# Graph attention with residual norm on one Trainium2 core: VectorE adds the first two products with v in tiles 11 to 15 too

## The chip, the core and the metric

The kernel runs on one core of a Trainium2 chip. The core has five engines that run side by side, each with its own instruction queue: TensorE (PE, matrix products and transposes, with its weight load PEld), VectorE (DVE), ScalarE (ACT), GpSimd (POOL, which here issues the gathers) and SyncE (SP, which issues DMAs). They wait for each other on semaphores. The metric is the device time of one execution in microseconds (us).

## The reference

One layer: attention over the edges of a graph of 4096 nodes, width 512, 8 heads of 64, then a feed-forward block and a last layer norm. `adj` is about 0.4% full, so a node has some 17 neighbours.

```python
hs = layer_norm(h_source); ht = layer_norm(h_target)          # h_source is x
q = (ht @ Wq + bq).reshape(T, H, HD) / jnp.sqrt(HD)
k = (hs @ Wk + bk).reshape(S, H, HD)
v = (hs @ Wv + bv).reshape(S, H, HD)
logits = jnp.where(edge_mask[None] != 0, jnp.einsum('thd,shd->hts', q, k), NEG)
ctx = jnp.einsum('hts,shd->thd', softmax(logits), v).reshape(T, D)
ht = layer_norm(ht + ctx @ Wo + bo)
out = layer_norm(x + ht + gelu(ht @ W1) @ W2)
```

All of it is float32.

## The kernel before

**Sorted targets, gathered edges.** The attention is not dense. The first part of the run turns each row of `adj` into a list of neighbours, projects `x` to k and v (one row of 1024 floats per node, in `kvd` in DRAM) and sorts the 4096 targets by degree in two halves of 2048. A tile is 128 targets of like degree, one on each partition. The tile's cap is the largest number of neighbours that it makes room for. The first half (`CAPS_A`, 16 tiles) is worked on while the lists of the second half (`CAPS_B`) are still being made. `_order` puts the tiles into groups of two; counted in the order of work, tiles 0 to 15 are the first half with caps 11, 13, 14, 15, 15, 16, 17, 17, 18, 19, 19, 20, 22, 23, 24, 39, and tile 16 (cap 12) is the first of the second half. `NA` is 16. Groups are [0], [1, 2], and so on: [11, 12], [13, 14], [15, 16].

**A step.** A tile is worked in steps of up to three neighbours (`S = 3`, list `SG`). For each neighbour slot POOL gathers 128 rows of k and v, one per partition, into `kv`, a ring of 17 places in the first half and 20 in the second (`RING`). `request` and `issue` do this four or five steps ahead (`AHEAD`). Then

- DVE multiplies the k halves by the query (line 1223) and sums each head (line 1228): the logits;
- ACT takes the exponential (lines 1232 and 1241, no maximum is subtracted) and, in a step of three, multiplies the third slot's v half by its weights itself (`by_scalar`, line 1207);
- DVE multiplies the v halves of the other slots by their weights (`values`, line 1184);
- PE adds the slots up: it transposes each 128x128 block of each slot by a product with the identity, and the transposes of all slots of a tile accumulate in one PSUM bank, `cps` (line 1195). Four transposes per slot.

From tile `NA` on, DVE adds slot 1 to slot 0 first (line 1188), and PE then transposes slot 0 and the third slot alone. From tile 21 on (`DENSE`), in every other step of three, DVE adds the third slot as well (line 1191).

**Around the steps.** `front` makes a tile's query (transposes, then the product with Wq, line 1012, then line 1017 on DVE). `finish` normalises a finished tile, multiplies it by Wo (line 1116) and prepares the feed-forward input `h2T`. `feed` runs the feed-forward block of a group (lines 1328 and 1337, PE) and adds its result on DVE (line 1284).

**What sets the order.** `attention` and `feed` are generators. `_weave` runs them by turns after hand-set costs (60 for a group of two), so that the feed-forward block of an earlier group is interleaved with the attention steps of a later one. A scheduler in the framework then fixes the order of each engine's queue at build time; each queue runs strictly in that order.

Of `values`, the lines that count:

```python
nc.vector.tensor_tensor(v4, v4, p[...].to_broadcast([P, m, H, HD]), ALU.mult)     # line 1184
slots = list(range(n))
if m > 1 and i >= NA:
    nc.vector.tensor_add(kv[:, 0, D:], kv[:, 0, D:], kv[:, 1, D:])                 # line 1188
    slots.remove(1)
```

Here `n` is the number of slots of the step and `m` the number that DVE multiplies: `n - 1` in a step of three, else `n`.

Of the kernel before, what the change touches and what calls it, by code (L numbers as in the profile page):

```python
# [443 lines left out]
def adj_resnorm_kernel(  # L444
# [56 lines left out]
    NA, NBT = len(CAPS_A), len(CAPS_B)  # L501
# [31 lines left out]
    with tc.tile_pool(name="keep", bufs=1) as keep:  # L533
# [17 lines left out]
        with ExitStack() as late:  # L551
# [489 lines left out]
            def request(k):  # L1041


                ahead = AHEAD + (1 if k >= first_b else 0)
                while issued[0] <= min(k + ahead, len(SG) - 1):
# [121 lines left out]
            def attention():  # L1167
# [10 lines left out]
                def values(i, j0, n, kv, p, cps, after):  # L1178

                    m = n - 1 if n == S else n
                    v4 = kv[:, :m, D:].rearrange("p j (h d) -> p j h d", h=H)
                    nc.vector.tensor_tensor(v4, v4, p[:, j0:j0 + m, :].unsqueeze(3)  # L1184
                                            .to_broadcast([P, m, H, HD]), ALU.mult)
                    slots = list(range(n))
                    if m > 1 and i >= NA:
                        nc.vector.tensor_add(kv[:, 0, D:], kv[:, 0, D:], kv[:, 1, D:])
                        slots.remove(1)
                        if n == S and i >= DENSE and j0 // S % 2:  # L1190
                            nc.vector.tensor_add(kv[:, 0, D:], kv[:, 0, D:], kv[:, S - 1, D:])
                            slots.remove(S - 1)
                    for j in slots:
                        for c in range(KC):
                            nc.tensor.matmul(cps[:, c, :], kv[:, j, D + c * P:D + (c + 1) * P], ident,  # L1195
                                             is_transpose=True, start=j0 + j == 0 and c == 0,
                                             stop=j0 + n == TILES[i][1] and j == slots[-1],
                                             skip_group_check=True)
                    if after is not None:
                        tails.append(after)  # L1200
# [11 lines left out]
                for group in GROUPS:  # L1212
# [3 lines left out]
                    for i in group:  # L1216
                        cps = ps.tile([P, KC, P], F32, name="cps", bufs=2)
                        while k < len(SG) and SG[k][0] == i:
# [16 lines left out]
                            if pend:  # L1235
                                values(*pend.pop())
                                request(k)
# [9 lines left out]
                            yield cost * n  # L1247
                            k += 1
                values(*pend.pop())
                while tails:  # L1250
                    advance()
# [130 lines left out]

            WAIT = 40.0
            AHEAD = 4
            DENSE = 21
            UNIT = 60.0

# [103 lines left out]
```

## Time and profile before

| | us |
|---|---|
| median of 3 runs | 1815.97 |
| lowest and highest | 1810.59 and 1816.34 |
| the profiled execution, its own time | 1805.6 |
| its span (first to last instruction) | 1803.7 |

Some rows of the profile for the operations of a step (whole run; a duration is from an instruction's start to its end, and neighbours on one engine can overlap):

| line, engine | what | count | mean ns | busy us |
|---|---|---|---|---|
| 1223 DVE | k times query | 211 | 1674 | 351.5 |
| 1228 DVE | sum of heads | 211 | 1665 | 350.1 |
| 1184 DVE | v times weights | 211 | 1192 | 250.9 |
| 1188 DVE | slot 1 added to slot 0 | 101 | 682 | 68.7 |
| 1207 ACT | third slot's v times weights | 1520 | 336 | 390.4 |
| 1195 PE | transposes into `cps` | 1896 | 281 | 252.3 |
| 1328 PE | feed-forward, first product | 2176 | 368 | 465.6 |
| 1337 PE | feed-forward, second product | 1024 | 598 | 466.3 |
| 967 POOL | gathers of k and v | 603 | 1276 | 769.3 |

How to read such a profile: busy time is an average over stages with different limits, so a stage has to be looked at by itself. "Idle before, releaser" names what the engine was waiting for. A wait on an engine that is not the bottleneck costs nothing. Attention runs from about 300 us to 1690 us of the span; before it come the lists and the projections, after it the rest of the feed-forward blocks.

### The profile page before, as it was taken

The page shows a single profiled execution, that of the slowest core. Times are in us where ns is not written, and L with a number is a line of the kernel's source. Part 1 is how long each engine was busy: PE and PEld are TensorE (multiplying, and loading weights), DVE is VectorE, ACT ScalarE, POOL GpSimd, SP SyncE. Part 2 cuts the span into 40 slices and gives each one's busy share as a digit, 9 for nine tenths or more (in the row PEclk, how much of TensorE's full clock was granted, in tenths as well). Part 3 has the DMA queues.
Part 4 walks back from the last instruction along what each step waited for, and adds up shares of the span by engine and source line. Part 5 has one row for each costly group of instructions (what it writes and reads, how often), then busy time and mean ns, then how long its engine had stood idle before and what let it go on. Part 6 is the DMA issues. An engine that isn't in the chain of part 4 may idle for free. (4 is left out here: it accounts for less than half of the span.)

```text
span 1803.7 us, 22807 instructions
## 1 busy us (share of the span) xinstructions
PE 1666.8 (92%) x6918; PEld 1085.7 (60%) x6918; DVE 1452.4 (81%) x2688; ACT 1229.2 (68%) x3125; POOL 994.7 (55%) x834
## 2 busy tenths in 40 slices
PE   7989994597999979999999989999899999999997
PEld 3444442475766656776776756666566666666664
DVE  6999886899999837777979989978797898998200
ACT  5767554487987646767778868877787776887311
POOL 1000145666566676776677788877575757773101
PEclk9999997698999989999999999999999999999998
DMA  9999969989797647777879878786787867684000
GB/s 343 370 385 372 344 215 326 401 282 339 259 313 254 203 162 255 252 255 260 286 260 313 291 261 296 253 280 231 235 263 240 285 212 268 218 287 154 16 9 26
DMA packets 140268, 463.25 MB, mean 257 GB/s; under 512 B 16500, under 2 KB 21672, under 8 KB 140136
## 3 DMA queue, kind: packets, MB, share of 16 engines
q0 software_dynamic: 96656, 342.64, 56.1%
q1 hardware_dynamic: 35664, 95.98, 15.1%
q10 hardware_dynamic: 7816, 23.08, 3.3%
q8 instruction: 57, 0.93, 0.2%
q14 instruction: 75, 0.61, 0.1%
HBM read 430.75 MB, written 30.89 MB: 256 GB/s over the span
## 5 line engine op out<-in xcount | busy, mean ns | idle before, releaser
L967 POOL DMA_INDIRECT kv<-kvd,rec x603 | 769.3, 1276 | 340.3 <-PE cps L1195 138.1
L1337 PE MATMUL po<-w,gt 128*128 128x512 f32 x1024 | 466.3, 598 | 16.7 <-ACT gt L1331 16.7
L1328 PE MATMUL pf<-h2T,w 128*128 128x256 f32 (+1 forms) x2176 | 465.6, 368 | 0.3 <-ACT h2T L1147 0.3
L1328 PEld LDWEIGHTS pf<-h2T,w 128*128 128x128 f32 x2176 | 389.1, 191 | 64.4 <-issue 19.8
L1223 DVE TENSOR_TENSOR kv<-kv,tq 128x1536 f32<-128x1536 f32 (+2 forms) x211 | 351.5, 1674 | 61.8 <-DMA kv<-kvd,rec 53.3
L1207 ACT ACTIVATE kv<-kv,pa 128x64 f32<-128x64 f32 x1520 | 390.4, 336 | 4.1
L1228 DVE TENSOR_REDUCE lg<-kv 128x24 f32<-128x1536 f32 (+2 forms) x211 | 350.1, 1665 | 1.1
L1337 PEld LDWEIGHTS po<-w,gt 128*128 128x128 f32 x1024 | 188.6, 192 | 212.8 <-issue 194.2
L1195 PEld LDWEIGHTS cps<-ident,kv 128*128 128x128 f32 x1896 | 227.9, 145 | 110.1 <-issue 45.5
L1195 PE MATMUL cps<-ident,kv 128*128 128x128 f32 x1896 | 252.3, 281 | 44.2 <-DVE kv L1184 36.5
L1184 DVE TENSOR_TENSOR kv<-kv,p 128x1024 f32<-128x1024 f32 (+1 forms) x211 | 250.9, 1192 | 14.4 <-ACT p L1232 14.1
L687 POOL TENSOR_TENSOR n_rs<-n_ve,mhalf 128x2 f32<-128x2 f32 (+2 forms) x51 | 49.9, 979 | 322.6 <-DVE n_ve L680 170.8
L729 ACT ACTIVATE kv<-kv 128x1024 uint8<-128x1024 int32 x128 | 134.9, 1056 | 93.9 <-DMA kv<-in_adj_dram 41.4
L1331 ACT ACT_TABLE_LOAD x106 | 136.0, 1283 | 1.8
L1331 ACT ACTIVATE gt<-pf 128x512 f32<-128x512 f32 x128 | 76.4, 597 | 88.0 <-PE pf L1328 84.5
L736 DVE MAX8 cand<-kv 128x8 uint16<-128x103 uint16 (+1 forms) x640 | 131.4, 251 | 0.6
L930 PE MATMUL pq<-wk,h2T 128*128 128x512 f32 x256 | 120.8, 616 | 11.8 <-ACT tq L932 6.3
L1012 PE MATMUL t<-wq,tq 128*128 128x512 f32 x256 | 120.5, 615 | 8.2 <-ACT tq L1006 8.2
L930 PE MATMUL pq<-wv,h2T 128*128 128x512 f32 x256 | 115.4, 593 | 2.1 <-ACT kv L932 1.7
L1116 PE MATMUL t<-wo,rb 128*128 128x512 f32 x256 | 115.2, 593 | 0.0
L1232 ACT ACTIVATE p<-lg 128x24 f32<-128x24 f32 (+2 forms) x179 | 39.1, 218 | 105.5 <-DVE lg L1228 104.7
L930 PEld LDWEIGHTS pq<-wk,h2T 128*128 128x128 f32 x256 | 48.8, 197 | 69.8 <-issue 50.1
(161 smaller groups left out, 1606.2 us busy)
## 6 DMA issues: line engine op xcount, KB each, us to landing
kv<-in_adj_dram SPq DMA_DIRECT2D x128, 512.0 KB, 7.0
kvd<-tq ACTq DMA_DIRECT2D x24, 512.0 KB, 6.4
kv<-kvd,rec POOLq DMA_INDIRECT x603, 5.9
kv<-in_L_gnn_h_target_dram SPq DMA_DIRECT2D x32, 256.0 KB, 7.4
kv<-in_x_dram SPq DMA_DIRECT2D x15, 512.0 KB, 8.8
rest_d<-gid SPq DMA_DIRECT2D x32, 160.0 KB, 4.8
w<-in_L_gnn_W_dram SPq DMA_DIRECT2D x4, 1024.0 KB, 10.3
kvd<-kv ACTq DMA_DIRECT2D x8, 512.0 KB, 5.8
```

The source lines that it names most:

```text
L729: nc.scalar.activation(sg, a, AF.Sign, accum_out=dpart[:, i, h:h + 1])
L736: nc.vector.max(cand[:, h * SQ + s, :], wd[:, w0:w1])
L930: nc.tensor.matmul(pkv, hT[:, kc, j * P:(j + 1) * P], w[:, kc, :], start=kc == 0, stop=kc == KC - 1)
L967: nc.gpsimd.indirect_dma_start(out=dst, out_offset=None, in_=table[:, :], in_offset=bass.IndirectOffsetOnAxis(ap=idx, axis=0))
L1184: nc.vector.tensor_tensor(v4, v4, p[:, j0:j0 + m, :].unsqueeze(3) .to_broadcast([P, m, H, HD]), ALU.mult)
L1195: nc.tensor.matmul(cps[:, c, :], kv[:, j, D + c * P:D + (c + 1) * P], ident, is_transpose=True, start=j0 + j == 0 and c == 0, stop=j0 + n ...
L1207: newest[:] = [nc.scalar.mul(v, v, pa[:, hd:hd + 1]).ins]
L1223: nc.vector.tensor_tensor(kv[:, :n, :D], kv[:, :n, :D], tq[:, :D].unsqueeze(1).to_broadcast([P, n, D]), ALU.mult)
L1228: nc.vector.tensor_reduce(lg[:, :n, :], kv[:, :n, :D].rearrange("p j (h d) -> p j h d", h=H), AX.X, ALU.add)
L1328: nc.tensor.matmul(pf[:, k, :], w1[(f0 + k) // KC][:, kc, (f0 + k) % KC * P:((f0 + k) % KC + 1) * P], h2T[:, kc, :w], start=kc == 0, stop= ...
L1331: nc.scalar.activation(gt, pf, AF.Gelu_apprx_tanh)
L1337: nc.tensor.matmul(po[j], gt[:, k, j * P:(j + 1) * P], w2[(f0 + k) // KC][:, (f0 + k) % KC, :], start=False, stop=f0 + k == FC - 1, skip_g ...
```

## The change

The add of line 1188 starts at tile 11 instead of tile 16. A new constant names the tile.

```diff
@@ values
                     slots = list(range(n))
-                    if m > 1 and i >= NA:
+                    if m > 1 and i >= ADDS:
                         nc.vector.tensor_add(kv[:, 0, D:], kv[:, 0, D:], kv[:, 1, D:])
                         slots.remove(1)
                         if n == S and i >= DENSE and j0 // S % 2:
@@ constants
             AHEAD = 4
+            ADDS = 11
             DENSE = 21
```

`ADDS` is set further down in the kernel than `values` stands, but before the generators run, like `DENSE`. Tiles 11 to 15 have caps 20, 22, 23, 24 and 39.

## The prediction

> **What bounds the kernel now.** I read the page's first two parts for the overall load, then cut the span by the first exponential of each tile (line 1241 on ScalarE's timeline: tile 11 at 754.6 us, tile 13 at 850.3, tile 15 at 936.7, tile 17 at 1040.8, tile 19 at 1140.2, tile 21 at 1227.6, tile 23 at 1316.1, tile 25 at 1400.9) and took the busy time of each engine in each stretch, one stretch being one group of two tiles. Last came the timelines of PE and DVE around the tile borders.
>
> The page: span, load, and the 40 slices of PE and DVE.
> ```profile
> span 1803.7 us, 22807 instructions
> ...
> PE 1666.8 (92%) x6918; PEld 1085.7 (60%) x6918; DVE 1452.4 (81%) x2688; ACT 1229.2 (68%) x3125; POOL 994.7 (55%) x834
> ...
> PE   7989994597999979999999989999899999999997
> DVE  6999886899999837777979989978797898998200
> ```
> PE carries the most, and the last three slices have PE alone (DVE falls to 2, 0, 0): the feed-forward part of the last groups. PE's order is fixed, so whatever the middle gains or loses on PE arrives at the end undiminished.
>
> The busy time by group; columns are stretch, length, then busy microseconds and instructions of PE, weight load, DVE, ACT and POOL, granted clock, DMA share and rate.
> ```profile
> core 0: us, PE busy (x) PEld busy (x) DVE busy (x) ACT busy (x) POOL busy (x), PEclk, DMA share, GB/s
> 754.60:850.30 95.70, 92.86 (x436) 65.19 (x435) 74.59 (x84) 66.19 (x183) 67.48 (x56) 1.00 0.77 260
> 850.30:936.70 86.40, 85.31 (x406) 59.50 (x405) 76.81 (x76) 70.18 (x202) 61.01 (x51) 1.00 0.81 275
> 936.70:1040.80 104.10, 101.14 (x488) 72.89 (x486) 89.48 (x84) 80.31 (x224) 78.58 (x66) 0.98 0.90 302
> 1040.80:1140.20 99.40, 91.15 (x408) 62.81 (x407) 92.82 (x97) 74.68 (x213) 83.03 (x58) 0.98 0.82 271
> 1140.20:1227.60 87.40, 83.71 (x358) 56.40 (x357) 76.20 (x86) 64.70 (x172) 64.44 (x55) 0.98 0.78 266
> 1227.60:1316.10 88.50, 82.72 (x332) 54.02 (x331) 74.44 (x87) 66.55 (x174) 57.91 (x45) 0.96 0.72 234
> 1316.10:1400.90 84.80, 83.47 (x353) 56.09 (x352) 74.05 (x85) 68.66 (x182) 59.30 (x49) 1.00 0.78 258
> ```
> The first three rows are tiles 11 to 16, where the change falls: PE is busy 279.3 of 286.2 us and bounds them; DVE, at 240.9, has 45.3 us to spare. The next rows already have the adds. There PE leaves 3.7 to 8.3 us of a group idle in three rows out of four.
>
> **The skill and the trace.** "VectorE: DVE Perf Modes", section "The TRN2 errata — SBUF-src ops pay a fixed extra latency per instruction", gives the fp32 add as (N+151)/0.96, which for 512 elements is 691 ns; line 1188 shows a median of 682 ns (653 to 729), so it agrees. "TensorE: Matmul & The Clock Gate", section "Step-by-step: what each phase is for", says that one matmul's drain overlaps the next one's fill, so that a stream is priced by its start-to-start gap and not by the listed duration. The trace agrees (0.109 us of gap beside 273 ns of median duration, below). The same page, section "HAM oscillation — how this bites in real kernels", warns of PE gaps over about 3.4 us, after which the clock is throttled; the trace has such a case, a 5.01 us wait shown further down.
>
> **Part 1, what goes: transposes.** Line 1188 joins slots 0 and 1 of a step, and the loop at line 1195 then leaves out slot 1: four 128x128 transposes fewer per step. The tiles concerned have caps 20, 22, 23, 24 and 39; in steps of three slots that is 7, 8, 8, 8 and 13 steps, of which one (tile 12's last, one slot) has nothing to add: 43 steps, 14 + 16 + 13 by group. Tile 16, the other half of the third group, has the adds already. The price of a transpose, from PE's timeline in tile 15:
> ```profile
> 950.39 1.47 PE L1195 MATMUL cps<-ident,kv 128*128 128x128 f32 x12
> 951.70 0.60 PE L1099 MATMUL t<-ident,rb 128*128 128x128 f32 x4
> ```
> Twelve take 951.70 - 950.39 = 1.31 us from start to start, 0.109 each, 0.437 for four. So PE loses 43 x 0.437 = 18.8 us of work (172 transposes; their weight loads go with them, beside the matmuls): 6.1, 7.0 and 5.7 us by group.
>
> **Part 2, what comes: adds on DVE.** DVE's timeline in tile 17, which has them:
> ```profile
> 1057.09 1.22 DVE L1184 TENSOR_TENSOR kv<-kv,p 128x1024 f32<-128x1024 f32 x1
> 1058.22 1.75 DVE L1228 TENSOR_REDUCE lg<-kv 128x24 f32<-128x1536 f32 x1
> 1059.88 0.68 DVE L1188 TENSOR_TENSOR kv<-kv 128x512 f32<-128x512 f32 x1
> 1060.48 1.75 DVE L1223 TENSOR_TENSOR kv<-kv,tq 128x1536 f32<-128x1536 f32 x1
> ```
> An add holds DVE for 1060.48 - 1059.88 = 0.60 us. 43 x 0.60 = 25.8 us more of DVE work: 8.4, 9.6 and 7.8 by group. The other thing to see: the add does not follow its multiply; a reduce of another step stands between. PE's operand is ready at 1060.56 instead of 1058.31, 2.25 us later, not 0.60. Nothing else is issued: no DMA, no queue is passed. The gather on POOL that refills slot 1 will wait for DVE's add instead of PE's transpose, which is earlier; I price that at nothing (the gathers in tiles 11 to 16 waited 25.0 us for PE in all).
>
> **Part 3, the new waits.** PE waits for the add before the step's first transpose, and behind that wait stands all of PE's queue, feed-forward included. Where DVE is far ahead, this is free. At the start of a tile it is not, as the border of tiles 12 and 13 shows on the two timelines:
> ```profile
> 838.48 3.60 PE L1012 MATMUL t<-wq,tq 128*128 128x512 f32 x8
> ...
> 856.57 1.53 PE L1195 MATMUL cps<-ident,kv 128*128 128x128 f32 x12 [1.09 <-DVE kv L1184]
> ```
> ```profile
> 842.12 0.69 DVE L1017 SCALAR_TENSOR_TENSOR tq<-t,bqr 128x512 f32<-128x512 f32 x1 [8.59 <-PE t L1012]
> ...
> 853.62 1.76 DVE L1223 TENSOR_TENSOR kv<-kv,tq 128x1536 f32<-128x1536 f32 x1 [3.01 <-DMA kv<-kvd,rec]
> ```
> DVE cannot start a tile before PE has made its query (line 1012), and PE's first transposes of the tile come 14.5 us after that; the chain between them is already 1.09 us too long here. At the borders 11/12 and 14/15 the multiply was ready only 1.05 and 3.41 us before the transposes. An add that comes 0.6 to 2.3 us later turns these into waits of about 1 to 3 us, four or five times. Against that, some of DVE's idle time goes: the 8.59 us above is a wait for PE, and shrinks as PE's queue shortens.
>
> **The sum.** New loads by group, PE: 92.86 - 6.1 = 86.8; 85.31 - 7.0 = 78.3; 101.14 - 5.7 = 95.5. DVE: 74.59 + 8.4 = 83.0; 76.81 + 9.6 = 86.4; 89.48 + 7.8 = 97.3. The larger of the two: 86.8, 86.4, 97.3, together 270.5 us. A group never takes only that. Length over larger load in the rows above is 1.031, 1.013, 1.029 for the three groups without adds, where PE's load is 11 to 24% above DVE's, and 1.071, 1.044, 1.070, 1.016 for the four with them, where the loads are 2 to 13% apart. After the change they are 2 to 10% apart, so I take 1.06, near the upper end of the second set, since the row that is closest to balance (2%) has 1.071: 270.5 x 1.06 = 286.7 us against 286.2 now, +0.5. Bounds: 1.03 gives 278.6 (-7.6), 1.071 gives 289.7 (+3.5). PE's gain is eaten because DVE takes its place as the busiest engine in the second and third group. On its own time the profiled execution goes from 1805.6 (span 1803.7 and 1.9 around it) to about 1806. The median shown, 1815.97, is 10.4 above that execution, so I forecast 1816.
>
> **Rivals.**
> - PE stays the bound. For it: inside tiles 11 to 14 DVE's lead over PE, from a multiply's end to the first transpose of its step, grows from 1 to 6 us at the start to 14 to 20 at the end (tile 14's last step: multiply done at 931.1, transposes from 945.6), and a tile of eight steps takes only 8 x (0.60 + 0.437) = 8.3 us from it. Against: the second group's DVE load, 86.4, is all of its present length. A ratio of 1.02 gives 275.9, -10: 1806 on the median's scale. The whole 18.8 would leave DVE no idle time (266.7 of 267.4).
> - Slower, by the borders: PE waits long enough at a tile's start for its clock to drop. The price is seen in tile 17:
> ```profile
> 1068.86 1.04 PE L1195 MATMUL cps<-ident,kv 128*128 128x128 f32 x8
> ...
> 1084.29 1.97 PE L1195 MATMUL cps<-ident,kv 128*128 128x128 f32 x8 [5.01 <-DVE kv L1188]
> ```
> Eight transposes took 1.97 us after the wait instead of 1.04, and the eight of line 1143 after them 1.75 instead of 1.04: 5.0 + 0.9 + 0.7 = 6.6 us. At the five starts of tiles 12 to 16 that makes 33, less 18.8: +14, 1830. It decides from waits of about 3 us on; with 1 to 2 us the forecast holds.
> - The change is not what it says: the index 11 counts tiles in the order of work, and 11 to 15 are the last five of the first part, so this is nearly excluded; or the generated instruction order comes out otherwise than in tile 17. No time of its own, no difference.
>
> **Chances.** Balanced engines, the forecast: 0.46 (own range -5.5 to +5.5 us, 1810 to 1822). PE-bound gain: 0.22. Border waits: 0.30. Not as it says: 0.02. About 0.3%, 5.4 us, is what a measurement can tell from no change. Of the forecast's share 0.02 falls below and 0.04 above that; so faster 0.24, same 0.42, slower 0.34. The range runs from 1803 (13 below, short of the full PE gain) to 1833 (17 above, the border waits and a little more).
>
> **What would show it.** Right: 172 fewer matmuls in line 1195's row, line 1188 at 144 instead of 101, PE's busy time lower by about 19 us but its idle time in tiles 11 to 16 up by as much; DVE's waits for gathers and for line 1012 gone; PE waits put down to line 1188. Wrong: PE gaps unchanged in that stretch (the first rival), or PE waits over 3 us with a lower clock (the second), or gains and losses after tile 17, where nothing is changed.

## The result, and the profile after

| | before | after |
|---|---|---|
| median of 22 runs each, us | 1815.63 | 1805.36 |
| lowest to highest | 1805.62 to 1821.21 | 1797.58 to 1814.58 |
| the profiled execution, its own time | 1805.6 | 1800.29 |

The ratio, of the means (1806.2 to 1814.6), is 0.9954, 95% interval [0.9938, 0.9969]: 0.46% faster. The forecast was no change; the time lies inside its range.

The page of the changed kernel, its load and two groups of instructions (line, engine, operation, count, busy us, mean ns, idle time before):
```profile
span 1798.6 us, 22490 instructions
...
PE 1653.8 (92%) x6746; PEld 1069.0 (59%) x6746; DVE 1472.5 (82%) x2731; ACT 1228.0 (68%) x3123; POOL 998.1 (55%) x834
...
L1195 PE MATMUL cps<-ident,kv 128*128 128x128 f32 x1724 | 235.7, 283 | 55.7 <-DVE kv L1184 25.1
...
L1188 DVE TENSOR_TENSOR kv<-kv 128x512 f32<-128x512 f32 x144 | 98.1, 683 | 0.3
```
The work is what was forecast: 172 matmuls fewer, 43 adds more. PE's busy time fell by 13.0 us and not by 19: a matmul's listed end is modelled, and matmuls that run at a lower clock count longer. The count by start-to-start distance, further down, gives 18.4 us.

Busy time by group in the changed kernel (tiles 11 and 12, 13 and 14, 15 and 16):
```profile
core 0: us, PE busy (x) PEld busy (x) DVE busy (x) ACT busy (x) POOL busy (x), PEclk, DMA share, GB/s
758.30:845.90 87.60, 86.83 (x380) 58.81 (x379) 82.03 (x98) 66.54 (x182) 61.99 (x54) 1.00 0.81 280
845.90:944.50 98.60, 92.10 (x403) 63.13 (x402) 88.45 (x94) 75.84 (x212) 75.93 (x59) 0.97 0.82 277
944.50:1034.80 90.30, 85.34 (x377) 57.88 (x377) 89.68 (x92) 74.22 (x213) 74.04 (x59) 0.98 0.88 307
```
The stretch of tiles 11 to 16 takes 276.5 us; before, it took 286.2. That is -9.7. The second group got longer, the first and third much shorter: work moved between groups as well. A caution on such figures: up to the start of tile 11 the two traces show the same sequence of operations on each engine, and still the changed kernel gets there 3.7 us later in its profiled execution (758.3 against 754.6; at tile 0 it was 2.7 behind). So a few us between two single executions mean nothing. Of the -9.7, -5.1 is left in the spans.

PE's and DVE's timelines at the borders of tiles 12/13 and 14/15 (start, duration, engine, line, then in brackets the idle time before it and what ended it):
```profile
834.99 3.70 PE L1012 MATMUL t<-wq,tq 128*128 128x512 f32 x8 [0.66 <-ACT tq L1006]
...
856.88 1.97 PE L1195 MATMUL cps<-ident,kv 128*128 128x128 f32 x8 [5.66 <-DVE kv L1188]
...
949.73 1.97 PE L1195 MATMUL cps<-ident,kv 128*128 128x128 f32 x8 [3.07 <-DVE lg L1228]
```
```profile
838.73 0.69 DVE L1017 SCALAR_TENSOR_TENSOR tq<-t,bqr 128x512 f32<-128x512 f32 x1 [1.68 <-PE t L1012]
...
851.61 1.82 DVE L1223 TENSOR_TENSOR kv<-kv,tq 128x1536 f32<-128x1536 f32 x1 [5.41 <-issue]
```
DVE's 8.59 us wait for the query has become 1.68. In return PE now waits 5.66 us for the add at this border, and its clock drops: the next eight transposes take 1.97 us instead of 1.04, and the granted clock of the group is 0.97, not 1.00. The same happens after 3.07 us of idle at the next group's start. So there are new losses, and still the stretch is shorter.

What DVE waited for in tiles 11 to 16, the entries for gathers and queries, first before, then after (total us, times, longest):
```profile
DVE kv L1223 <- DMA kv<-kvd,rec: 20.2, 9, 7.4
DVE tq L1017 <- PE t L1012: 8.8, 2, 8.6
```
```profile
DVE kv L1223 <- issue: 6.2, 2, 5.4
...
DVE tq L1017 <- PE t L1012: 1.7, 1, 1.7
...
DVE kv L1223 <- DMA kv<-kvd,rec: 0.3, 1, 0.3
```
The waits for gathers went from 20.2 us to 6.5 (the 6.2 before line 1223 have no releaser in the records, but stand at the same place). The diff touches neither gathers nor queries, except that a gather into slot 1's place now waits for DVE's add and no longer for PE (theory C below). What did change besides is the order of the queues: the build schedules all engines anew, and from tile 11 on PE's, DVE's, ACT's and POOL's queues differ from those of before.

### The profile page after: what moved, and what is told of

The parts are those of the page before. It is cut to its first block, busy times and chain, and to the rows that moved or that the text cites. A ratio compares the mean times of both kernels' runs of the same rounds, so it can differ in the third digit from the quotient of the medians.

```text
span 1798.6 us, 22490 instructions
## 1 busy us (share of the span) xinstructions
PE 1653.8 (92%) x6746; PEld 1069.0 (59%) x6746; DVE 1472.5 (82%) x2731; ACT 1228.0 (68%) x3123; POOL 998.1 (55%) x834
## 5 line engine op out<-in xcount | busy, mean ns | idle before, releaser
L1195 PE MATMUL cps<-ident,kv 128*128 128x128 f32 x1724 | 235.7, 283 | 55.7 <-DVE kv L1184 25.1
L1195 PEld LDWEIGHTS cps<-ident,kv 128*128 128x128 f32 x1724 | 209.5, 147 | 124.1 <-issue 55.4
L1188 DVE TENSOR_TENSOR kv<-kv 128x512 f32<-128x512 f32 x144 | 98.1, 683 | 0.3
```

## The experiments

Four theories. A: PE bounds tiles 11 to 15, and the gain is the transposes less what the adds cost. B: the gain comes from the new order of the queues. C: the add frees slot 1's ring place earlier than the transposes did, and the gathers profit. G, formed after the first eight runs: the look-ahead of the gathers bounds these tiles together with PE.

A table first. "PE work" in tiles 11 to 16 counts matmuls by their usual distance from start to start (0.109 us a 128x128 block, 0.216 for 256 columns, 0.429 for 512); "PE idle" is what the actual distances have beyond it, so it holds PE's waits and also what a lower clock after a wait adds. Both, and the stretch, come from one profiled execution each. The sum of the two is a little under the stretch, since distances within 0.05 us of the usual one count as work.

| kernel | ratio to before | 95% interval | tiles 11 to 16, us | PE work | PE idle |
|---|---|---|---|---|---|
| before | 1 | | 286.2 | 276.3 | 9.7 |
| the change | 0.9954 | 0.9938 to 0.9969 | 276.5 | 257.9 | 18.1 |
| pe_only | 0.9998 | 0.9983 to 1.0013 | 289.1 | 257.1 | 31.6 |
| dve_only | 1.0063 | 1.0040 to 1.0086 | 300.6 | 275.9 | 24.2 |
| order_before_relief | 0.9999 | 0.9980 to 1.0017 | 290.5 | 257.5 | 32.8 |
| order_before_change | 1.0106 | 1.0090 to 1.0123 | 307.0 | 256.2 | 50.5 |
| order_after_relief | 0.9866 | 0.9850 to 0.9882 | 261.6 | 257.5 | 3.5 |
| order_after_work_before | 1.0177 | 1.0155 to 1.0200 | 311.9 | 276.3 | 35.3 |

**One half of the change at a time.** `pe_only` leaves slot 1 out in tiles 11 to 15: no transposes, no add; the output lacks these neighbours there. This work is called relief below.
```diff
-                    if m > 1 and i >= NA:
-                        nc.vector.tensor_add(kv[:, 0, D:], kv[:, 0, D:], kv[:, 1, D:])
+                    if m > 1 and i >= ADDS:
+                        if i >= NA:
+                            nc.vector.tensor_add(kv[:, 0, D:], kv[:, 0, D:], kv[:, 1, D:])
                         slots.remove(1)
```


> Tiles 11 to 15 leave slot 1 out of the sum altogether: no transposes for it and no add either, so the output lacks one neighbour in three there. Theory A (PE bounds these tiles, the change is worth its 172 transposes less what the adds cost): all of 43 x 0.437 = 18.8 us comes through, ratio about 0.990 to before, and the difference to the changed kernel, some 9 us, is the price of the adds. Theory B (the gain comes from the rearranged instruction order, not from the work removed): no relation to 18.8, anything from 0.985 to 1.005. Theory C (the gain is the earlier release of slot 1 to the gathers): the same as the changed kernel or a little better, 0.993 to 0.996.

Measured: 0.9998. Taking 19 us of work from an engine that was busy 98% of the stretch gives nothing: A asked for 0.990 and falls in this plain form. DVE's and PE's waits in `pe_only`, tiles 11 to 16 (where lines after 1188 have a number one higher):
```profile
DVE kv L1224 <- DMA kv<-kvd,rec: 28.7, 13, 7.1
DVE tq L1017 <- PE t L1012: 8.1, 1, 8.1
...
DVE kv L1224 <- issue: 2.9, 1, 2.9
```
```profile
PE cps L1196 <- DVE kv L1184: 11.5, 3, 7.3
PE t L1012 <- ACT tq L1006: 8.2, 3, 6.5
```
What left PE came back as waiting: DVE for gathers, PE for DVE's multiplies and for the query's input. PE's idle time rose from 9.7 to 31.6 us. Theory C falls here too: the ring place of slot 1 is free even earlier than with the add, yet the waits for gathers grew from 20.2 to 31.6 us.

`dve_only` makes the adds and keeps all transposes; the sum goes to the k half of slot 0, which is no longer read.
```diff
+                    if m > 1 and ADDS <= i < NA:
+                        nc.vector.tensor_add(kv[:, 0, :D], kv[:, 0, D:], kv[:, 1, D:])
-                    if m > 1 and i >= ADDS:
+                    if m > 1 and i >= NA:
```


> Tiles 11 to 15 do the 43 adds on VectorE, but into the dead k half of slot 0, and PE still transposes all three slots: VectorE's load without PE's relief and without a new wait for PE; the output is right. Theory A: VectorE has 45 us to spare in these tiles, so 25.8 us more cost 0 to 5 us, ratio 1.000 to 1.003. Theory B: an order of its own, anything within 1% either way. Theory C: slot 1 is still released by PE, so no gain, 1.000.

Measured: 1.0063, 11.4 us slower by the ratio; 14.4 in the stretch. A's 1.000 to 1.003 was too low. In the trace PE runs the same sequence of operations as in the kernel before; the orders of DVE, ACT and POOL differ. `twice` is the changed kernel with a second add per step, into the dead k half of slot 1:
```diff
                         nc.vector.tensor_add(kv[:, 0, D:], kv[:, 0, D:], kv[:, 1, D:])
+                        if i < NA:
+                            nc.vector.tensor_add(kv[:, 1, :D], kv[:, 0, :D], kv[:, 1, :D])
```


> The changed kernel with a second add of the same size in each of the 43 steps of tiles 11 to 15 (k halves, never read): VectorE's load there rises by another 25.8 us to about 286 us, the length of the stretch before the change. Theory A: VectorE is then the bound alone, the stretch takes about 1.03 x 286 = 295 us, so 9 us more than before the change and 18 more than the changed kernel, ratio 1.005. If VectorE still has room (PE is the bound after the change): no more than 3 us over the changed kernel, 0.997.

Measured: 1.0018 [1.0004, 1.0032], 0.64% above the change and between the two forecasts. So the adds are not free, although DVE had 45 us to spare. In the profile the stretch takes 300.3 us, 23.8 more than in the change, and what comes after it 754.6 instead of 763.8: what the middle loses does not arrive "undiminished" at the end, as the prediction had it. Then two other starts for the adds, `ADDS = 13` and `ADDS = 9`:

> The add starts at tile 13 instead of 11: 29 adds instead of 43, 12.7 us of PE work less than before. Theory A with the gain spread as the traces show it (about 3 us each in tiles 11, 15 and 16, little in 12 to 14): 5 to 6 us, ratio 0.997. Theory A with every tile alike: 29/43 of the changed kernel's gain, 0.997 too. Theory B: anything within 0.5% of before, not in order with the number of adds.

> The changed kernel with the adds from tile 9 on instead of tile 11. If the gain goes with the transposes taken from TensorE (theory A, in the new order), two tiles more give about as much again per tile as five gave: 0.993 to 0.995. adds13 (three tiles) gave 0.9986 and five gave 0.9954. If each build's order is a draw (theory B), the number has no relation to that line: 0.990 to 1.006.

Measured: 0.9986 [0.9970, 1.0002] and 0.9990 [0.9977, 1.0003]. Three tiles give next to nothing, five give 0.46%, seven give nothing: no line by tile, as A wants it. `adds9` takes 276.0 us for tiles 11 to 16, as the change does, but its tiles 9 and 10, which have adds too, take 116.9 us where the change takes 108.3.

**The same work in another order.** In these kernels the order of the four queues PE, ACT, DVE and POOL is written out: the instructions of an engine are chained ("pinned") as recorded from another build, by order edges without a wait.
```diff
+        for a, b in zip(seq, seq[1:]):
+            tc.add_manual_dep(b, a.name, mybir.DependencyInfo(mybir.DependencyClass.NoSync,
+                                                              mybir.DependencyReason.DATA),
+                              reason="order")
```
`order_before_change` is the changed work in the order of before, each add straight after its multiply; in `order_before_change_late` one DVE instruction stands between.

> The changed kernel's work, but every queue of PE, ScalarE, VectorE and GpSimd is pinned to the order of the kernel before; the 172 transposes are taken out where they stood and each add stands right behind its multiply. Theory A (the work removed from PE makes the gain, less what the adds cost): the gain is kept or is larger, since the adds come earlier: ratio 0.990 to 0.996. Theory B (the gain comes from the order that the build chose for the changed kernel): no gain, 0.999 to 1.004.

> The same, with one VectorE instruction between each multiply and its add, as the build places them by itself. Theory A: 0.992 to 0.998, slower than the one with the adds at once by what the later adds make PE wait, 2 to 6 us in all (0.001 to 0.003). Theory B: 0.999 to 1.006. If the place of the add doesn't matter: the same as the other within 0.001.

Measured: 1.0106 and 1.0109 [1.0090, 1.0127]. The same arithmetic that is 0.46% faster in its own order is 1.06% slower in the old one. A's ranges are missed, and both times lie above B's as well: the old order does not merely lose the gain. Whether the add stands at once or one instruction later makes no difference here. `order_before_relief` leaves slot 1 out as `pe_only` does, in the order of before:

> Slot 1 is left out of the sum in tiles 11 to 15 (no transposes, no add), in the order of the kernel before, pinned; the output lacks these neighbours. The kernel pe_only has the same work in an order of its own and took 0.9998. Theory A with its stalls as a matter of order: PE's 18.8 us come through here at least in part, 0.990 to 0.995. If something else than PE bounds these tiles (gathers, the chain through VectorE and ScalarE): 0.998 to 1.001, as pe_only.

Measured: 0.9999. Again nothing for 19 us of PE. No run pins a kernel to its own order, so what pinning costs by itself was not measured; that this run agrees with `pe_only`, and that the fastest kernel below is pinned, speaks against much. `order_after_work_before` is the reverse: the full work of before in the order of the changed kernel (all but 8 of POOL's instructions kept to it).

> The work of the kernel before (all transposes, no adds in tiles 11 to 15), pinned to the order of the changed kernel; the transposes of slot 1 stand behind those of slot 0. Theory A: no gain, 0.999 to 1.003. Theory B: the changed kernel's gain, 0.994 to 0.997.

Measured: 1.0177. The new order is bad for the old work, and B, which asked for the change's gain here, falls in this form. (The places of slot 1's transposes were set by hand, so this is not an order that a build chose.) Last, `order_after_relief` leaves slot 1 out in the new order, so that it differs from `pe_only` in order alone, and from the changed kernel in the adds alone:

> The first two products are left out in tiles 11 to 15 (no transposes of theirs, no add: the output lacks these neighbours there), with the instruction order of the changed kernel written out by hand. Set beside the changed kernel it prices the 43 adds alone, in the order that won. If VectorE's load sets tiles 11 to 15 in that order (its busy time stood above TensorE's in the second and fourth groups after the change), taking some 26 us of adds away must give a good part of it: 0.985 to 0.991. If the order itself, with its waits from engine to engine, sets it, the adds are nearly free there: 0.993 to 0.997. A ratio near 1.000 would say that even this order is worth something only with the adds in it.

Measured: 0.9866, in the range for adds that are not free: they cost 0.89% in this order. (The text above says DVE's busy time stood above PE's in the second group; by the table of the changed kernel it did so in the third, and in the second PE's was higher.) The busy time by group, with the columns of above, first of `pe_only`, then of `order_after_relief`:
```profile
751.90:846.50 94.60, 88.13 (x380) 59.48 (x379) 73.97 (x84) 66.68 (x183) 67.46 (x59) 0.96 0.81 279
846.50:939.30 92.80, 88.81 (x386) 60.52 (x385) 77.37 (x78) 70.50 (x200) 64.57 (x52) 0.98 0.81 270
939.30:1041.00 101.70, 88.35 (x390) 60.32 (x390) 86.75 (x83) 80.05 (x224) 77.41 (x61) 0.97 0.84 282
```
```profile
756.70:843.00 86.30, 86.30 (x380) 58.87 (x379) 74.56 (x84) 66.60 (x182) 60.95 (x55) 1.00 0.82 288
843.00:931.10 88.10, 85.90 (x384) 58.79 (x383) 79.08 (x77) 75.25 (x213) 66.36 (x58) 1.00 0.89 304
931.10:1018.30 87.20, 86.79 (x393) 59.47 (x392) 82.90 (x79) 73.95 (x211) 70.95 (x59) 1.00 0.93 321
```
The same instructions take 289.1 us in one order and 261.6 in the other. In the second PE is busy without a gap in the first group, and its clock stays at 1.00. Of the three orders in which slot 1 was left out, only in this one is PE the bound. DVE's waits there (its line 1348 is 1223 of before, 1137 is 1017):
```profile
DVE kv L1348 <- issue: 7.9, 3, 4.3
...
DVE tq L1137 <- PE t L1132: 3.8, 2, 3.5
...
DVE kv L1348 <- DMA kv<-kvd,rec: 1.6, 3, 1.0
```
9.5 us for gathers instead of 31.6 (7.9 of them again without a releaser), 3.8 for the query instead of 8.1. These two waits do not explain every order, though. `order_before_change` has less of them than the kernel before, and takes 307.0 us; what PE waits for most there is the query's input from ACT (first DVE, then PE; lines 1353, 1141 and 1136 are 1223, 1017 and 1012 of before):
```profile
DVE kv L1353 <- DMA kv<-kvd,rec: 15.1, 5, 7.2
DVE tq L1141 <- PE t L1136: 6.9, 2, 6.6
```
```profile
PE t L1136 <- ACT tq L1130: 11.9, 4, 4.6
```
The six ratios side by side (1 and 0.9954 are in the order of their own build, the others pinned):

| work in tiles 11 to 15 | order of before | order of the change |
|---|---|---|
| all transposes, no adds | 1 | 1.0177 |
| relief: slot 1 left out | 0.9999 | 0.9866 |
| adds in place of slot 1's transposes | 1.0106 | 0.9954 |

Relief alone gives nothing, the new order alone costs 1.8%, and both together give 1.3%; the adds then cost 0.9 to 1.1% in either order.

**A wider ring.** `ring11_before` and `ring11_after` use the ring of 20 places and the longer look-ahead from tile 11 on, not from 16.
```diff
+            WIDE = 11
-                if place[-1] + n > RING[i >= NA]:
+                if place[-1] + n > RING[i >= WIDE]:
-            first_b = next(k for k, (i, _, _) in enumerate(SG) if i >= NA)
+            first_b = next(k for k, (i, _, _) in enumerate(SG) if i >= WIDE)
```


> The kernel before with the ring of 20 places and one more step of look-ahead already from tile 11 on instead of tile 16. Nothing else of the work changes. If the look-ahead of the gathers bounds tiles 11 to 15 beside TensorE (theory G: this is why relieving TensorE alone gave nothing), it gains: 0.992 to 0.997. If gathers do not bound there, the build only draws another order for the same work: 0.998 to 1.004, and the spread of such a redraw is what this run then shows.

> The changed kernel with the ring of 20 places and one more step of look-ahead from tile 11 on. Theory G (gathers bound beside TensorE, so that part of the 18.8 us that left TensorE is still lost to them): 0.985 to 0.992. Theory B alone (the order fits the work or does not): anything from 0.993 to 1.003, with no link to the size of the ring.

Measured: 0.9934 [0.9915, 0.9953] and 0.9924 [0.9900, 0.9948]. The first lies in G's range, the second between G's and B's. Both are clearly faster than before; that they are also below the change is not clear of the error, since the intervals overlap. With the wider ring the change is worth 0.10%, which is within the error. `ring11_relief` joins the wider ring and `pe_only` (the same neighbours missing):

> The first two products left out in tiles 11 to 15 (no transposes, no add: these neighbours are missing from the output), with the ring of 20 places and the longer look-ahead from tile 11 on, in the build's own order. Left out with the ring of 17 the ratio was 0.9998, the wider ring alone gave 0.9934. If gathers and TensorE bound these tiles together (theory G), both reliefs together give more than their sum of 0.66%: 0.980 to 0.988. If they are two draws of the order: 0.990 to 0.998.

Measured: 0.9931 [0.9909, 0.9952], as the wider ring without relief. Theory G asked for 0.980 to 0.988 and falls in this form.

**Mere redraws.** Here the planner's cost `UNIT` is 61 in place of 60, for steps and feed alike, so that the build draws another order for the same work. (The two expectations below speak of 62 from tile 10 on; what ran is the edit shown. Its orders differ from about 375 us on, those of the change from its before only from tile 11 on, so the nudge redraws more than the edit does.)
```diff
-            UNIT = 60.0
+            UNIT = 61.0
```


> The kernel before with no work changed: only the planner's cost for the steps of the groups from tile 10 on is 62 in place of 60, so that the build draws another order. It prices a mere redraw of the order. If a redraw is worth as much as the change (theory B as a lottery), the ratio may lie anywhere in 0.990 to 1.010; if redraws move little and the order has to fit the moved work, it stays in 0.998 to 1.002.

> The changed kernel with the same nudge of the planner's cost (62 in place of 60 in the groups from tile 10 on). If the gain of 0.46% belongs to the work moved, it survives another order: 0.993 to 0.997. If it was the luck of one order: anything in 0.990 to 1.006, as likely above 0.998 as below.

Measured: 1.0048 [1.0028, 1.0069] and 1.0023 [1.0008, 1.0038]. A redraw moves the time by as much as the change does, with nothing added or removed; this also means that the wider ring's 0.66% can't be put down to its places. Of its own two cases, the second run fits "the luck of one order". Between the two redraws the change is worth 1.0023/1.0048 = 0.9975, with the two intervals joined about 0.995 to 1.000.

**One queue held.** The changed work, with only some queues held in the order of before and the rest scheduled by the build around them; the edit is the chain above, for those engines alone.

> The changed work, with GpSimd's queue alone (which issues the gathers) held in the order of the kernel before; the build orders the other engines around it. The changed work in the old order of all four queues gave 1.0106, in its own order 0.9954. If the place of the gathers in GpSimd's queue carries the difference (theory G): 1.003 to 1.011. If it is the order on TensorE and VectorE that carries it: 0.993 to 0.999.

> The changed work with VectorE's queue alone held in the order of the kernel before (each added add comes one instruction after its multiply); the build orders the other engines around it. It is the control to the run that held GpSimd's queue alone (1.0119). If the place of the gathers in GpSimd's queue is what carries the difference (theory G), holding VectorE instead must leave GpSimd free to gain: 0.994 to 1.001. If holding any one queue spoils a plan that fits as a whole (theory B), it costs about as much: 1.005 to 1.013.

> The changed work with TensorE, ScalarE and VectorE held in the order of the kernel before and GpSimd's queue left to the build. All four held gave 1.0106. If GpSimd's order alone carries the difference (theory G): 0.995 to 1.002. If the old order on the other three engines is what costs (theory B): 1.007 to 1.013.

Measured: POOL held 1.0119 [1.0095, 1.0142]; DVE held 0.9991 [0.9976, 1.0006]; PE, ACT and DVE held and POOL free 1.0057 [1.0040, 1.0075]. The first two fit G's numbers within the error; the third lies between the two ranges. But in tiles 11 to 16 the first two take 293.9 and 294.6 us, the same; they part later, in tiles 17 to 24 (375.0 against 348.3 us), where no work was changed. Which queue carries the difference stays open.

## Why the prediction was wrong

**"PE is busy 279.3 of 286.2 us and bounds them": half true.** PE's work is one limit of the stretch (276 us), but there is a second one right beside it: with 19 us less PE work the stretch still takes 290.5 us in the old order and 289.1 in the order that the build drew for this work. The busy share could not show it. The Trainium skill, "Perfetto Trace Analysis", section "Identifying the Most-Contended Engine", says that matmul busy time is not a good measure of the distance to the roofline, and to take, among others, the share of weight loads. That share was 69% here (197.6 of 286.2), which fits a PE with room. But it doesn't tell the cases apart: it is 68% (177.1 of 261.6) in `order_after_relief`, where PE has 3.5 us of gaps and does bound. The count by start-to-start distance tells them apart, but only once the work is left out: PE then idles for 31.6 us in `pe_only` and for 3.5 here. The 9.7 us of the kernel before gave no warning.

**Part 1, 18.8 us of PE work: right.** It went from 276.3 to 257.9 us.

**Part 2, 25.8 us of DVE work: the size right, its cover wrong.** DVE's busy time rose by 23.8 us (1472.5 against 1448.7 in `order_after_relief`) or 28.0 (1481.0 against 1453.0, order of before). The 45 us to spare did not take it in: the adds raise PE's idle time in the stretch by 14.5 us (work of before, each in its build's order), 17.7 (order of before) and 14.6 (order of after). By the ratios they cost 0.63%, 1.07% and 0.89%, so 11 to 19 us. In the old order it did not matter that an add comes one instruction late.

**Part 3, waits at the borders: right in kind.** The two largest waits of PE in the stretch, in the changed kernel:
```profile
PE cps L1195 <- DVE kv L1188: 8.3, 5, 5.7
PE cps L1195 <- DVE lg L1228: 3.1, 1, 3.1
```
PE waited for the add five times, 8.3 us in all, and probably a sixth time: the second entry is the 3.07 us at tile 15, and an add ended 0.06 us before its end. The second rival's clock drop came at two borders and not at five. Its point of decision, about 3 us, is not a sharp one (last section).

**"The sum": the step that failed.** It said "so I take 1.06". Measured: the larger loads are 86.83, 92.10 and 89.68, together 268.6 (forecast 270.5), and the stretch is 276.5, a ratio of 1.029. The ratio is the term that was mis-sized: 268.6 x 1.06 would be 284.7. The group nearest to balance has 1.071, the other two 1.009 and 1.007. In the prediction's own sign, PE's idle time was to rise by as much as its work fell, 19 us; it rose by 8.4. DVE became the busiest engine in the third group alone, not in the second. Beneath the number lay the assumption that the ratio follows from how close two loads are. The prediction's own rows hardly bore that out (1.070 with loads 11% apart, 1.044 with 10%), and the runs show that it depends on the order: the same work, relief, has 3.5 or 31.6 us of PE idle. What happened, as a sum that the runs show step by step: relief in its own build, 0; the changed kernel's order in place of that one, 0.9998 to 0.9866, some -24 us; the adds in it, 0.9866 to 0.9954, some +16. It is -8 in all.

**The rival "PE stays bound" had the number (1806) and not the cause.** Its sign was unchanged gaps of PE; PE's idle time about doubled, from 9.7 to 18.1 us. That the number fits is luck, all the more since the change under a nudged planner lies at 1.0023.

**Is it a gain of the change?** With the same build settings on both sides the change gives -0.46%, -0.25% (redraws) and -0.10% (wider ring); the last two are hardly or not told from nothing. The sign is the same three times, but held in the old order the change costs 1.06%, so the size, and there the sign too, belongs to the order. Shown is that neither the relief nor the new order gains by itself, and that both together do. In the two pairs looked at (before and the change, `pe_only` and `order_after_relief`) the shorter stretch is the one in which DVE waits less for gathers and queries; `order_before_change` shows that other waits can cost as much. Which wait leads, and why the build's plan fits better with the adds in it, was not shown.

## What to carry to other kernels

Before a cost is moved off an engine that is 98% busy, leave the work out altogether and run that: if nothing comes, as in `pe_only`, a second limit stands beside the first in that order of the queues. It does not prove that the move can't gain: here the same relief gave 1.3% in another order, and the change, which does more work than `pe_only`, came out 0.46% faster. Where a scheduler orders in-order queues, every edit draws a new order: compare an effect of half a per cent with what a neutral nudge of the planner does (here +0.48% and +0.69%), or hold the order fixed. And an order that is good for one work need not be good for another: the changed work in the old order was 1.1% slower than before, the old work in the new order 1.8%.

## What was not expected of the hardware

How long PE has to idle before its transposes run slower has no sharp point in these traces. An idle time of 2.75 us in `pe_only` was followed by eight transposes in 1.97 us, as were 3.07 and 5.66 us in the changed kernel; after 3.10 us in `dve_only` twelve took 1.53, and the products behind them ran at full speed too:
```profile
867.90 1.97 PE L1196 MATMUL cps<-ident,kv 128*128 128x128 f32 x8 [2.75 <-DVE kv L1184]
```
```profile
858.59 1.53 PE L1197 MATMUL cps<-ident,kv 128*128 128x128 f32 x12 [3.10 <-DVE kv L1184]
859.96 0.60 PE L1099 MATMUL t<-ident,rb 128*128 128x128 f32 x4
860.40 3.60 PE L1339 MATMUL po<-w,gt 128*128 128x512 f32 x8
```
The Trainium skill, "TensorE: Matmul & The Clock Gate", section "HAM oscillation — how this bites in real kernels", puts the limit at about 3.4 us; here shorter waits were enough, but not always.

And 1.3% hung on the order alone: the same work, relief, has the ratio 0.9866 in `order_after_relief` and 0.9998 in `pe_only`.
